# LoRA rows of the first conditioning layer fetched per batch row by indirect DMA onto quarters of the partitions, in place of masked expert tables

## The chip, the core and the metric

The program runs on one core of a Trainium2 chip, in one launch. The metric is device time in microseconds (us) of that core, from the first to the last instruction as the device counts it. The kernel before takes 626.87 us, the median of three runs (626.77 to 627.61).

## The reference, cut to what matters

`x` has 8 batch rows of 256 positions with 128 features. Two residual layers follow each other; each is a conditioning step and then a feed-forward block:

```
x = x + L0_ffn(L0_cond(x, itok_B_0_7))     # expert id 0..7 for each batch row
x = x + L1_ffn(L1_cond(x, itok_B_0_3))     # language id 0..3 for each batch row
```

The change touches `L0_cond` only. With D = 128, F = 512, rank 16 for the common and for each expert's part, and ALPHA = 2, it computes for a batch row b with expert e:

```
h = relu(x wi^T + 2 (x common_wi_a^T) common_wi_b^T + 2 (x experts_wi_a[e]^T) experts_wi_b[e]^T)
y =      h wo^T + 2 (h common_wo_a^T) common_wo_b^T + 2 (h experts_wo_a[e]^T) experts_wo_b[e]^T
```

`L0_ffn` is four rounds of a top-2 mixture of four experts (128 to 512 to 128, gelu), and it holds most of the arithmetic. `L1_cond` is a small LoRA by language, and `L1_ffn` is a gated block with two 512 x 512 layers.

## The kernel before

Activations lie with features on the 128 partitions and positions along the free axis, in four tiles t = 0..3 of 512 positions (`NT`), so that a tile holds two batch rows (`BPT`). All matrices are float32. A float32 matmul appears in the profile as two records ("passes"), each with its own weight load.

`L0_cond` does not multiply x by the low-rank factors one after the other. It makes merged dense weights for each batch row and multiplies by those:

- Common part, once: `pc_i` (L125) and `pc_o` (L130) multiply the common factors, contracting over 16 partitions; VectorE adds the dense weights and gives `wie` (L126) and `woe` (L131).
- Expert part: the factors of all eight experts lie below each other on 128 partitions (8 x 16 rows). `emask` (L110) is 2 where a partition belongs to the expert of batch row b and 0 elsewhere. VectorE masks the up table, eight times (`wam`, L146); GpSimd masks the down table, eight times (`wobm`, L162).
- `up_weights(b)` (L148): one matmul `pwi` (L150, contracting over 128 partitions, 512 columns) and one VectorE addition of `wie` (L152) give the up weights of one batch row. `down_weights(g)` (L160): four matmuls `pwo` (L165, 512 columns) and four additions (L168) give the down weights of four batch rows.
- `cond_up(t)` (L172) multiplies x by the up weights, two batch rows at 256 columns each for four chunks of 128 (`phc`, L178), and ScalarE applies relu. `cond_down(t)` (L185) sums four chunks for each batch row (`po`, L190), and VectorE copies the result to `cur[t]` (L194).

After that, `gate` (L199) computes the routing of a tile: `pg` matmuls (L207, L210), a chain of small VectorE operations with a tanh on ScalarE, transposes `pt` (L255) with the identity `ident`, and a broadcast on GpSimd (L261). `experts` (L264) runs the mixture for one tile and one round: `ph` (L269) with gelu (L273), and `py` (L283). Sixteen such steps follow each other, then the last layers.

What orders the work: each engine runs its instructions in one order fixed at build time. The tile framework assigns buffers from pools and inserts semaphore waits; a scheduler interleaves the instructions of neighbouring calls. PSUM (matmul results) is split into pools of 512-column banks: `ps_mm` with three, `ps_y` with two, `ps_bc` with two, `ps_g` with one. Loads are issued from the SyncE queue (SPq) and the ScalarE queue (ACTq). On GpSimd (POOL) the order at the start is: a memset of `ident`, a memset of the first `cwq`, an instruction of `masks.py:199` that reloads the library of GpSimd programs (it has no row of its own in the profile), the affine select that completes `ident`, the second `cwq`, the eight masks of L162, and then casts of later weights (L322).

Of the kernel before, what the change touches and what calls it, by code (L numbers as in the profile page):

```python
# [31 lines left out]

V_B1, V_B2, V_W1S, V_W2S, V_H1S, V_H2S, V_W3S, V_N = 0, 16, 20, 24, 28, 32, 36, 37

C_EIDX, C_PIDX, C_UPPER, C_N = 0, 1, 2, 18


@with_exitstack
def body(ctx: ExitStack, tc: tile.TileContext, a: dict, outT: bass.AP):

    nc = tc.nc

    w = ctx.enter_context(tc.tile_pool(name="w", bufs=1))
    act = ctx.enter_context(tc.tile_pool(name="act", bufs=1))
    hp = ctx.enter_context(tc.tile_pool(name="hp", bufs=9))
    mid = ctx.enter_context(tc.tile_pool(name="mid", bufs=2))
    small = ctx.enter_context(tc.tile_pool(name="small", bufs=3))
# [12 lines left out]
    xs = [act.tile([P, NT], F32, tag=f"x{t}", name=f"x{t}") for t in range(T)]  # L60
    ids = w.tile([P, 2 * B], I32, tag="ids", name="ids")
    nc.scalar.dma_start(ids, a["ids"].partition_broadcast(P))
    cst = load("cst", nc.scalar)
    waR = load("waR", nc.sync)
    wbT = load("wbT", nc.sync)
    cwia = load("cwia", nc.scalar)
    cwibT = load("cwibT", nc.scalar)
    wiT = load("wiT", nc.sync)
    nc.sync.dma_start(xs[0], a["xT"][:, ts(0, NT)])
    cwoa = load("cwoa", nc.scalar)  # L70
    cwobT = load("cwobT", nc.scalar)
    wobT = load("wobT", nc.sync)
    woaR = load("woaR", nc.sync)
    woT = load("woT", nc.sync)
    for t in range(1, T):
        nc.sync.dma_start(xs[t], a["xT"][:, ts(t, NT)])
    wg = load("wg", nc.scalar)
# [24 lines left out]
    for k in range(2):  # L102
# [2 lines left out]

    idf = w.tile([P, 2 * B], F32, tag="idf", name="idf")
    nc.vector.tensor_copy(idf, ids)

    emask = w.tile([P, B], F32, tag="emask", name="emask")
    nc.vector.tensor_scalar(  # L110
        emask, idf[:, 0:B], cst[:, C_EIDX : C_EIDX + 1], 2.0, ALU.is_equal, ALU.mult
    )
# [10 lines left out]
    wie = w.tile([P, F], F32, tag="wie", name="wie")  # L123
    pc = ps_mm.tile([P, NT], F32, tag="mm", name="pc_i")
    nc.tensor.matmul(pc, lhsT=cwia, rhs=cwibT, start=True, stop=True)  # L125
    nc.vector.scalar_tensor_tensor(wie, pc, 2.0, wiT, ALU.mult, ALU.add)  # L126
    woe = w.tile([P, FC, D], F32, tag="woe", name="woe")
    pc = ps_mm.tile([P, FC, D], F32, tag="mm", name="pc_o")
    for c in range(FC):
        nc.tensor.matmul(pc[:, c, :], lhsT=cwoa[:, ts(c, P)], rhs=cwobT, start=True, stop=True)  # L130
    nc.vector.scalar_tensor_tensor(woe, pc, 2.0, woT, ALU.mult, ALU.add)  # L131

    def masked(dst, src, mask, t):
        for b in range(BPT):
# [5 lines left out]


    cur = [act.tile([P, NT], F32, tag=f"cur{t}", name=f"cur{t}") for t in range(T)]
    wam = hp.tile([P, B, D], F32, tag="h", name="wam")
    wobm = hp.tile([P, B, D], F32, tag="h", name="wobm")
    for b in range(B):
        nc.vector.tensor_scalar(wam[:, b, :], waR, emask[:, b : b + 1], None, ALU.mult)  # L146

    def up_weights(b):  # L148
        pw = ps_bc.tile([P, F], F32, tag="bc", name=f"pwi_{b}")
        nc.tensor.matmul(pw, lhsT=wam[:, b, :], rhs=wbT, start=True, stop=True)  # L150
        wt = mid.tile([P, F], F32, tag="wib", bufs=3, name=f"wib_{b}")
        nc.vector.tensor_tensor(wt, pw, wie, ALU.add)  # L152
        return wt

    GB = 4
    down_w = [
        hp.tile([P, FC, GB, D], F32, tag="h", name=f"wob{g}") for g in range(B // GB)
    ]

    def down_weights(g):  # L160
        for b in range(g * GB, (g + 1) * GB):
            nc.gpsimd.tensor_scalar(wobm[:, b, :], wobT, emask[:, b : b + 1], None, ALU.mult)  # L162
        for c in range(FC):
            pw = ps_bc.tile([P, GB, D], F32, tag="bc", name=f"pwo_{g}_{c}")
            nc.tensor.matmul(  # L165
                pw, lhsT=woaR[:, ts(c, P)], rhs=wobm[:, ts(g, GB), :], start=True, stop=True
            )
            nc.vector.tensor_tensor(  # L168
                down_w[g][:, c], pw, woe[:, c, :].unsqueeze(1).to_broadcast([P, GB, D]), ALU.add
            )  # L170

    def cond_up(t):  # L172
        wt = [up_weights(t * BPT + b) for b in range(BPT)]
        h = hp.tile([P, FC, NT], F32, tag="h", name=f"hc_{t}")
        for c in range(FC):
            ph = ps_mm.tile([P, NT], F32, tag="mm", name=f"phc_{t}_{c}")
            for b in range(BPT):
                nc.tensor.matmul(  # L178
                    ph[:, ts(b, S)], lhsT=wt[b][:, ts(c, P)], rhs=xs[t][:, ts(b, S)],
                    start=True, stop=True,  # L180
                )
            nc.scalar.activation(h[:, c, :], ph, AF.Relu)  # L182
        return h

    def cond_down(t, h):  # L185
        po = ps_y.tile([P, NT], F32, tag="y", name=f"po_{t}")
        for b in range(BPT):
            g, k = divmod(t * BPT + b, GB)
            for c in range(FC):
                nc.tensor.matmul(  # L190
                    po[:, ts(b, S)], lhsT=down_w[g][:, c, k, :], rhs=h[:, c, ts(b, S)],
                    start=(c == 0), stop=(c == FC - 1),
                )
        nc.vector.tensor_copy(cur[t], po)  # L194
# [69 lines left out]
    def experts(r, t, cwb):  # L264
# [36 lines left out]
        if r == R - 1:  # L301
            nc.vector.tensor_tensor(xs[t], xs[t], cur[t], ALU.add)

    before = cond_up(0)
    for t in range(1, T):
        if t % (GB // BPT) == 1:
            down_weights(t // (GB // BPT))
        h = cond_up(t)
        cond_down(t - 1, before)
        before = h  # L310
    cwb = gate(0, 0)
# [160 lines left out]
def _laid_out(i):  # L472

    import numpy as np

    i = {k: np.asarray(v) for k, v in i.items()}

    def cols(v):
        return v.reshape(-1, P).T

    def rows(m):
        return m.reshape(-1, P, m.shape[1]).transpose(1, 0, 2)

    cst = np.zeros((P, C_N), np.float32)
    cst[:, C_EIDX] = np.arange(P) // 16
    cst[:, C_PIDX] = np.arange(P)
    cst[:, C_UPPER:] = np.triu(np.ones((E, E), np.float32), 1).reshape(-1)
    arrays = {
        "xT": i["x"].reshape(N, D).T,
        "ids": np.concatenate([i["itok_B_0_7"], i["itok_B_0_3"]]),  # L490
        "cst": cst,
        "wiT": i["L0_cond_wi"].T,
        "woT": rows(i["L0_cond_wo"].T),
        "cwia": i["L0_cond_common_wi_a"],
        "cwibT": i["L0_cond_common_wi_b"].T,
        "cwoa": i["L0_cond_common_wo_a"],
        "cwobT": i["L0_cond_common_wo_b"].T,
        "waR": i["L0_cond_experts_wi_a"].reshape(P, D),
        "wbT": i["L0_cond_experts_wi_b"].transpose(0, 2, 1).reshape(P, F),
        "woaR": i["L0_cond_experts_wo_a"].reshape(P, F),  # L500
        "wobT": i["L0_cond_experts_wo_b"].transpose(0, 2, 1).reshape(P, D),
        "wg": i["L0_ffn_Wg"].transpose(1, 0, 2),
        "bg": i["L0_ffn_bg"].reshape(-1),
        "W1": i["L0_ffn_W1"].transpose(1, 0, 2),
        "W2": i["L0_ffn_W2"].reshape(E, FC, P, D).transpose(2, 0, 1, 3),
        "laT": i["L1_cond_lora_A"].reshape(LR, D).T,
        "lbT": i["L1_cond_lora_B"].transpose(0, 2, 1).reshape(LR, D),
        "lemb": i["L1_cond_lang_embed"],
        "w1T": i["L1_ffn_w1_w"].T,
        "w2T": i["L1_ffn_w2_w"].T,  # L510
        "h1T": rows(i["L1_ffn_h1_w"].T),
        "h2T": rows(i["L1_ffn_h2_w"].T),
        "w3T": rows(i["L1_ffn_w3_w"].T),
        "vecs": np.concatenate(
            [
                cols(i["L0_ffn_b1"].reshape(-1)),
                cols(i["L0_ffn_b2"].reshape(-1)),
                cols(i["L1_ffn_w1_s"]),
                cols(i["L1_ffn_w2_s"]),
                cols(i["L1_ffn_h1_s"]),  # L520
                cols(i["L1_ffn_h2_s"]),
                cols(i["L1_ffn_w3_s"]),
            ],
            axis=1,
        ),
    }
    return {k: np.ascontiguousarray(v) for k, v in arrays.items()}
# [21 lines left out]
```

## Time and profile before

| what | value |
|---|---|
| median of three runs | 626.87 us |
| the profiled execution: device time | 628.72 us |
| the profiled execution: span from first to last instruction | 626.9 us |
| granted TensorE clock over the span | 0.990 |
| TensorE (PE) busy | 607.5 us, 97% |
| VectorE (DVE) busy | 242.7 us, 39% |
| ScalarE (ACT) busy | 229.4 us, 37% |
| GpSimd (POOL) busy | 93.7 us, 15% |
| DMA traffic | 8.81 MB, of it 7.44 MB in the first 60 us |

A row of a timeline starts with the start in us and the duration in us; then come engine, line, operation, output and inputs, shape and count; brackets say how long the engine was idle before and what ended that. A row that joins several instructions counts passes, so "pwi x4" is two matmuls. A duration of a single TensorE row includes the latency of the pipeline; in a stream the pace is shorter than the row. The chain of waits is followed back from the last instruction of the kernel and lists what the end had to wait for, piece after piece.

The page has PE at nine tenths or more in nearly every slice after the first, so there are two places where time can go: the start, before PE has its inputs, and the amount of PE work itself.

### The profile page before, as it was taken

What the parts mean: (1) busy time and instruction counts of PE and PEld (TensorE: products, weight loads), DVE (VectorE), ACT (ScalarE), POOL (GpSimd) and SP (SyncE); (2) the same over time, 40 slices, a digit from 0 to 9 for tenths busy, and PEclk for the clock granted to TensorE, in tenths of its full rate; (3) what the DMA queues carried; (4) which work ended last, traced back from release to release, by engine and by line L of the source; (5) the groups of instructions that cost most, each with busy time, mean ns of one, the idle gap of its engine ahead of it and who ended that gap; (6) DMA issues with size and microseconds to landing.
All of it is one profiled execution on the core that took longest, in us unless ns stands there. A gap on an engine that the chain in (4) does not pass through costs nothing.

```text
span 626.9 us, 4871 instructions
## 1 busy us (share of the span) xinstructions
PE 607.5 (97%) x1758; PEld 317.6 (51%) x1758; DVE 242.7 (39%) x563; ACT 229.4 (37%) x344; POOL 93.7 (15%) x137
## 2 busy tenths in 40 slices
PE   4999999999999999999999999999999998899996
PEld 2667444444444444444444444444444343678885
DVE  3355158614141432424141424224243314766533
ACT  0213443343333425344433334253433342365431
POOL 3302100211010101010100101010101000444421
PEclk9999999999999999999999999999999998799999
DMA  7600000000000000000000000000000000000001
GB/s 225 248 1 1 1 1 0 1 0 1 1 0 0 1 0 1 2 0 1 1 0 0 1 0 0 2 0 0 1 0 0 1 1 0 1 1 17 1 17 38
DMA packets 4131, 8.81 MB, mean 14 GB/s; under 512 B 1284, under 2 KB 1640, under 8 KB 3592
## 3 DMA queue, kind: packets, MB, share of 16 engines
q1 hardware_dynamic: 3256, 8.33, 3.8%
q8 instruction: 16, 0.26, 0.2%
q10 hardware_dynamic: 848, 0.14, 0.1%
q14 instruction: 11, 0.09, 0.0%
HBM read 7.41 MB, written 1.05 MB: 13 GB/s over the span
## 4 chain that ended last, share of the span: by engine, by line
PE 94%; DMA 1%; DVE 1%; ACT 1%; issue 1%; POOL 0%; ACTq 0%; DVEq 0%; POOLq 0%
PE ph L269 35%; PE py L283 35%; PE pha_True L402 5%; PE phb_True L402 4%; PE phc L178 2%; PE po L190 2%; PE p_True L402 2%; PE pwi L150 1%; PE pt L255 1%; PE pwo L165 1%; PE pg L210 1%; PE pout_True L402 1%; PE pg L207 1%; DMA woT<-in_woT_dram 1%; DMA cwibT<-in_cwibT_dram 1%; PE pv L355 1%
## 5 line engine op out<-in xcount | busy, mean ns | idle before, releaser
L273 ACT ACTIVATE h<-ph,vecs 128x512 f32<-128x512 f32 x256 | 175.7, 687 | 278.5 <-PE ph L269 275.8
L269 PE MATMUL ph<-cur,W 128*128 128x512 f32 x512 | 232.8, 596 | 0.4 <-ACT h L273 0.4
L283 PE MATMUL py<-h,W 128*128 128x512 f32 x512 | 227.7, 592 | 0.0
L283 PEld LDWEIGHTS py<-h,W 128*128 128x128 f32 x512 | 97.1, 190 | 121.5 <-issue 121.3
L269 PEld LDWEIGHTS ph<-cur,W 128*128 128x128 f32 x512 | 94.5, 190 | 109.4 <-issue 106.8
L288 DVE SCALAR_TENSOR_TENSOR tmp<-py,vecs,cwb 128x512 f32<-128x512 f32 x48 | 36.0, 751 | 203.7 <-PE py L283 203.7
L261 POOL PARTITION_BROADCAST cwb<-cwT x64 | 45.3, 811 | 403.3 <-DVE cwT L257 403.3
L288 DVE SCALAR_TENSOR_TENSOR acc<-py,vecs,cwb 128x512 f32<-128x512 f32 x16 | 12.0, 750 | 62.1 <-PE py L283 62.1
L292 DVE TENSOR_TENSOR acc<-acc,tmp 128x512 f32<-128x512 f32 x48 | 33.4, 695 | 1.2
L402 PE MATMUL pha_True<-h_True,h1S 128*128 128x512 f32 x128 | 31.4, 400 | 0.0
L402 PE MATMUL phb_True<-ha_True,h2S 128*128 128x512 f32 x128 | 30.9, 392 | 0.0
L402 PEld LDWEIGHTS pha_True<-h_True,h1S 128*128 128x128 f32 x128 | 24.6, 192 | 5.9
L402 PEld LDWEIGHTS phb_True<-ha_True,h2S 128*128 128x128 f32 x128 | 23.8, 188 | 6.2 <-ACT fhb_True L441 0.8
L182 ACT ACTIVATE hc<-phc 128x512 f32<-128x512 f32 x16 | 9.3, 596 | 34.4 <-PE phc L178 34.3
L389 POOL CAST h_True<-f 128x512 fp32r<-128x512 f32 x16 | 13.1, 823 | 45.7 <-DVE f L426 45.6
L207 PE MATMUL pg<-wg,chi 128*128 128x8 f32 x64 | 19.4, 324 | 0.0
L390 DVE TENSOR_TENSOR hb_True<-fhb_True,hb_True 128x512 fp32r<-128x512 f32 x16 | 12.0, 764 | 15.6 <-POOL hb_True L389 15.5
L421 ACT ACTIVATE g_True<-p_True,vecs 128x512 f32<-128x512 f32 x16 | 10.8, 688 | 19.8 <-PE p_True L402 19.7
L390 DVE TENSOR_TENSOR ha_True<-fha_True,ha_True 128x512 fp32r<-128x512 f32 x16 | 11.4, 717 | 15.2 <-POOL ha_True L389 15.2
L441 ACT ACTIVATE fhb_True<-phb_True,vecs 128x512 f32<-128x512 f32 x16 | 10.7, 688 | 15.8 <-PE phb_True L402 13.1
L441 ACT ACTIVATE fha_True<-pha_True,vecs 128x512 f32<-128x512 f32 x16 | 10.9, 689 | 15.1 <-PE pha_True L402 12.5
L257 DVE COPY cwT<-pt 128x512 f32<-128x512 f32 x16 | 11.1, 691 | 13.8 <-PE pt L255 13.8
(99 smaller groups left out, 401.0 us busy)
## 6 DMA issues: line engine op xcount, KB each, us to landing
W<-in_W_dram SPq DMA_DIRECT2D x2, 1024.0 KB, 9.7
x<-in_xT_dram SPq DMA_DIRECT2D x4, 256.0 KB, 5.7
h1T<-in_h1T_dram SPq DMA_DIRECT2D x1, 1024.0 KB, 9.2
h2T<-in_h2T_dram SPq DMA_DIRECT2D x1, 1024.0 KB, 9.2
out_dram<-o_True SPq DMA_DIRECT2D x4, 256.0 KB, 2.5
wbT<-in_wbT_dram SPq DMA_DIRECT2D x1, 256.0 KB, 3.9
wiT<-in_wiT_dram SPq DMA_DIRECT2D x1, 256.0 KB, 4.5
woaR<-in_woaR_dram SPq DMA_DIRECT2D x1, 256.0 KB, 3.0
```

The source lines that it names most:

```text
L178: nc.tensor.matmul(ph[:, ts(b, S)], lhsT=wt[b][:, ts(c, P)], rhs=xs[t][:, ts(b, S)], start=True, stop=True,)
L207: nc.tensor.matmul(pg[:, j, :], lhsT=chi[:, ts(j, P)], rhs=wg2[:, r, :], start=True, stop=False)
L261: nc.gpsimd.partition_broadcast(cwb[:, e, :], cwT[q : q + 1, :], channels=P)
L269: nc.tensor.matmul(ph, lhsT=W1[:, e, ts(c, P)], rhs=cur[t], start=True, stop=True)
L273: nc.scalar.activation(h[:, c, :], ph, AF.Gelu_apprx_tanh, bias=vecs[:, col : col + 1])
L283: nc.tensor.matmul(py, lhsT=W2[:, e, c, :], rhs=h[:, c, :], start=(c == 0), stop=(c == FC - 1))
L288: nc.vector.scalar_tensor_tensor(dst, py, vecs[:, col : col + 1], cwb[:, e, :], ALU.add, ALU.mult)
L292: nc.vector.tensor_tensor(acc, acc, dst, ALU.add)
L389: nc.gpsimd.tensor_copy(dst[0][:, c, :], full)
L390: nc.vector.tensor_tensor(dst[1][:, c, :], full, dst[0][:, c, :], ALU.subtract)
L402: nc.tensor.matmul(out, lhsT=wT[c], rhs=part[:, c, :], start=(c == 0 and k == 0), stop=(c == n - 1 and k == len(src) - 1),)
L441: nc.scalar.activation(full, ph, AF.Gelu, scale=vecs[:, col : col + 1])
```

## The change

The host lays each expert table with the 16 common rows below it: `wa` and `woa` and so on are 144 rows long, 128 rows of eight experts and 16 common ones. `idr` holds for each partition the expert id of the batch row to which its quarter belongs (partition quarter k of 32 belongs to batch row 4g + k). VectorE computes from it the row of the table that each partition wants (`rows`): on the first 16 partitions of a quarter a row of the expert, on the other 16 a common row. For each of the two groups g of four batch rows GpSimd issues four indirect DMAs, which fetch one row for each partition.

Merged weights are then made by matmuls that contract over one quarter of 32 partitions (expert and common part together), one quarter for each batch row, and VectorE computes 2 x product + dense weight in one operation. The masks (`emask`, `wam`, `wobm`), the common products (`pc_i`, `pc_o`) and `wie`, `woe` are gone. For the up weights there are four matmuls of 512 columns in a group; for the down weights there are sixteen of 128 columns. Each batch row has a PSUM bank of its own, from `ps_bc` and `ps_y`.

In the changed GpSimd order the eight indirect DMAs stand behind the affine select and so behind the reload of the library, and ahead of the second `cwq` memset. Loads of eight small or middle-sized tables leave the SyncE and ScalarE queues; `wiT` moves to the ScalarE queue, and `ids` stands later in it.

```
-    ids = w.tile([P, 2 * B], I32, tag="ids", name="ids")
-    nc.scalar.dma_start(ids, a["ids"].partition_broadcast(P))
-    cst = load("cst", nc.scalar)
-    waR = load("waR", nc.sync)
-    wbT = load("wbT", nc.sync)
-    cwia = load("cwia", nc.scalar)
...
+    idr = w.tile([P, B // GB], I32, tag="idr", name="idr")
+    nc.sync.dma_start(idr, a["idr"])
+    cst = load("cst", nc.scalar)
+    nc.sync.dma_start(xs[0], a["xT"][:, ts(0, NT)])
+    wiT = load("wiT", nc.scalar)
+    woT = load("woT", nc.sync)
+
+    rows = w.tile([P, B // GB], I32, tag="rows", name="rows")
+    nc.vector.tensor_scalar(
+        rows, idr, cst[:, C_STEP : C_STEP + 1], cst[:, C_BASE : C_BASE + 1], ALU.mult, ALU.add
+    )
+    lora = {}
+    for g in range(B // GB):
+        for name in ("wa", "wb", "woa", "wob"):
+            src = a[name]
+            t = w.tile([P, src.shape[1]], F32, tag=f"{name}{g}", name=f"{name}{g}")
+            nc.gpsimd.indirect_dma_start(
+                out=t, out_offset=None, in_=src,
+                in_offset=bass.IndirectOffsetOnAxis(ap=rows[:, g : g + 1], axis=0),
+                bounds_check=src.shape[0] - 1,
+            )
+            lora[name, g] = t
...
+    up_w, down_w = {}, {}
+    banks = [(ps_bc, "bc"), (ps_bc, "bc"), (ps_y, "y"), (ps_y, "y")]
+
+    def merged(g, which):
+
+        pw = []
+        for k, (pool, tag) in enumerate(banks):
+            pw.append(pool.tile([P, F], F32, tag=tag, name=f"pw{which}_{g}_{k}"))
+        if which == "i":
+            for k in range(GB):
+                q = slice(k * RK, (k + 1) * RK)
+                nc.tensor.matmul(
+                    pw[k], lhsT=lora["wa", g][q, :], rhs=lora["wb", g][q, :], start=True, stop=True
+                )
+        else:
+            for c in range(FC):
+                for k in range(GB):
+                    q = slice(k * RK, (k + 1) * RK)
+                    nc.tensor.matmul(
+                        pw[k][:, ts(c, P)], lhsT=lora["woa", g][q, ts(c, P)],
+                        rhs=lora["wob", g][q, :], start=True, stop=True,
+                    )
+        dense = wiT if which == "i" else woT.rearrange("p c d -> p (c d)")
+        for k in range(GB):
+            b = g * GB + k
+            wt = mid.tile([P, F], F32, tag=f"w{which}b", bufs=4, name=f"w{which}b_{b}")
+            nc.vector.scalar_tensor_tensor(wt, pw[k], 2.0, dense, ALU.mult, ALU.add)
+            (up_w if which == "i" else down_w)[b] = wt
...
+    merged(0, "i")
     before = cond_up(0)
+    merged(0, "o")
     for t in range(1, T):
-        if t % (GB // BPT) == 1:
-            down_weights(t // (GB // BPT))
+        if t == GB // BPT:
+            merged(1, "i")
         h = cond_up(t)
+        if t == GB // BPT + 1:
+            merged(1, "o")
         cond_down(t - 1, before)
         before = h
```

Below, `pwi` and `pwo` of the changed kernel are the matmuls of `merged` for the up and the down weights; group 0 and group 1 are the two groups of four batch rows; RK = 32 and GB = 4.

More of the change, by code (lines that the diff above doesn't have):

```diff
@@ L33 @@
 V_B1, V_B2, V_W1S, V_W2S, V_H1S, V_H2S, V_W3S, V_N = 0, 16, 20, 24, 28, 32, 36, 37
-C_EIDX, C_PIDX, C_UPPER, C_N = 0, 1, 2, 18
+C_EIDX, C_PIDX, C_UPPER, C_STEP, C_BASE, C_N = 0, 1, 2, 18, 19, 20
+RK = 32
+GB = P // RK
 @with_exitstack
@@ L60, in body @@
     xs = [act.tile([P, NT], F32, tag=f"x{t}", name=f"x{t}") for t in range(T)]
+    idr = w.tile([P, B // GB], I32, tag="idr", name="idr")
[19 more added lines that the diff above has]
+            lora[name, g] = t
     ids = w.tile([P, 2 * B], I32, tag="ids", name="ids")
     nc.scalar.dma_start(ids, a["ids"].partition_broadcast(P))
-    cst = load("cst", nc.scalar)
-    waR = load("waR", nc.sync)
-    wbT = load("wbT", nc.sync)
-    cwia = load("cwia", nc.scalar)
[L67 to L74, printed above, removed]
     for t in range(1, T):
@@ L107, in body @@
     nc.vector.tensor_copy(idf, ids)
[L109 to L112, printed above, removed]
     lmask = w.tile([LR, B], F32, tag="lmask", name="lmask")
@@ L120, in body @@
     )
[L123 to L131, printed above, removed]
     def masked(dst, src, mask, t):
@@ L142, in body @@
     cur = [act.tile([P, NT], F32, tag=f"cur{t}", name=f"cur{t}") for t in range(T)]
[L143 to L170, printed above, removed]
+    up_w, down_w = {}, {}
@@ L172, in cond_up @@
     def cond_up(t):
-        wt = [up_weights(t * BPT + b) for b in range(BPT)]
         h = hp.tile([P, FC, NT], F32, tag="h", name=f"hc_{t}")
@@ L178, in cond_up @@
                 nc.tensor.matmul(
-                    ph[:, ts(b, S)], lhsT=wt[b][:, ts(c, P)], rhs=xs[t][:, ts(b, S)],
+                    ph[:, ts(b, S)], lhsT=up_w[t * BPT + b][:, ts(c, P)], rhs=xs[t][:, ts(b, S)],
                     start=True, stop=True,
@@ L187, in cond_down @@
         for b in range(BPT):
-            g, k = divmod(t * BPT + b, GB)
             for c in range(FC):
                 nc.tensor.matmul(
-                    po[:, ts(b, S)], lhsT=down_w[g][:, c, k, :], rhs=h[:, c, ts(b, S)],
+                    po[:, ts(b, S)], lhsT=down_w[t * BPT + b][:, ts(c, P)], rhs=h[:, c, ts(b, S)],
                     start=(c == 0), stop=(c == FC - 1),
@@ L486, in _laid_out @@
     cst[:, C_PIDX] = np.arange(P)
-    cst[:, C_UPPER:] = np.triu(np.ones((E, E), np.float32), 1).reshape(-1)
+    cst[:, C_UPPER : C_UPPER + E * E] = np.triu(np.ones((E, E), np.float32), 1).reshape(-1)
+    own = np.arange(P) % RK < 16
+    cst[:, C_STEP] = 16 * own
+    cst[:, C_BASE] = np.arange(P) % 16 + np.where(own, 0, 8 * 16)
     arrays = {
@@ L493, in _laid_out @@
         "woT": rows(i["L0_cond_wo"].T),
[L494 to L501, printed above, removed]
+        "idr": np.repeat(i["itok_B_0_7"].reshape(B // GB, GB).T, RK, axis=0),
+        "wa": np.concatenate([i["L0_cond_experts_wi_a"].reshape(P, D), i["L0_cond_common_wi_a"]]),
+        "wb": np.concatenate(
+            [i["L0_cond_experts_wi_b"].transpose(0, 2, 1).reshape(P, F), i["L0_cond_common_wi_b"].T]
+        ),
+        "woa": np.concatenate([i["L0_cond_experts_wo_a"].reshape(P, F), i["L0_cond_common_wo_a"]]),
+        "wob": np.concatenate(
+            [i["L0_cond_experts_wo_b"].transpose(0, 2, 1).reshape(P, D), i["L0_cond_common_wo_b"].T]
+        ),
         "wg": i["L0_ffn_Wg"].transpose(1, 0, 2),
```

## The prediction

> **What bounds the kernel now.** I read the page first: TensorE (PE) is busy for 97% of the span, and the chain of waits is PE for 94%. So I asked the chain of waits, in order of time, for the first 75 us, where all of the change lies.
>
> ```profile
> 2.12 4.60 DMA cwibT<-in_cwibT_dram
> ...
> 6.74 4.69 DMA woT<-in_woT_dram
> ...
> 11.52 0.69 DVE woe L131
> 12.21 0.32 DVE wam L146
> 12.53 0.04 issue
> 12.58 3.78 PE pwi L150 x4
> 16.36 2.80 PE phc L178 x12
> ...
> 23.65 1.91 PE pwi L150 x4
> 25.56 3.64 PE phc L178 x16
> 29.20 3.45 PE po L190 x16
> ```
>
> Up to 12.58 us loads are the bound; from there PE runs without a gap worth naming up to 59.28, where the mixture (`ph` L269) begins. After that the change alters no PE work. So the new time is the old one plus the shift of that point: the start of the first `pwi`, plus what PE does between it and `ph`. The first four `pwi` passes go at 0.945 us each (3.78 / 4), later ones at 0.43 (1.72 / 4): PE starts at half pace and is up to speed near 16.4.
>
> GpSimd is idle in most of the span, but the timeline of its first 30 us matters, because the fetches go there.
>
> ```profile
> 0.86 0.53 POOL L103 MEMSET cwq<- 128x512 f32 x1
> 10.47 0.28 POOL masks.py:199 TENSOR_SCALAR_AFFINE_SELECT ident<-ident 128x128 f32<-128x128 f32 x1 [9.08 <-issue]
> 10.72 0.51 POOL L103 MEMSET cwq<- 128x512 f32 x1
> 11.23 4.76 POOL L162 TENSOR_SCALAR wobm<-wobT,emask 128x128 f32<-128x128 f32 x8
> ```
>
> Between 1.39 and 10.47 GpSimd does nothing: the library reload ahead of the affine select takes these 9.1 us. In the changed order all eight indirect DMAs stand behind that select.
>
> Last, two rows of the PE and weight-load timelines for matmuls that do not use the array as others do: `pll` (L351) fills 64 columns of it, `pc_i` contracts over 16 rows only.
>
> ```profile
> 463.46 1.07 PE L351 MATMUL pll<-x,laT 128*64 128x512 f32 x2
> 464.46 2.84 PE L269 MATMUL ph<-cur,W 128*128 128x512 f32 x6
> ```
>
> ```profile
> 6.86 2.04 PE L125 MATMUL pc_i<-cwibT,cwia 16*128 16x512 f32 x2 [6.86 <-DMA cwibT<-in_cwibT_dram]
> 8.70 1.91 PE L130 MATMUL pc_o<-cwobT,cwoa 16*128 16x128 f32 x8
> ```
>
> **Part 1: what is removed.** `emask`, `wam` (8 x 0.25 us of VectorE), `wobm` (4.76 us of GpSimd), `pc_i`, `pc_o`, `wie` and `woe` all lie before 12.58 or beside PE. What they set is the start of `pwi` at 12.58, and part 2 puts another start in its place; nothing more is gained from them. The eight L152 and eight L168 additions (0.69 us each) become sixteen `scalar_tensor_tensor` of one size with `wie`'s row (0.69): no change for VectorE.
>
> **Part 2: the fetch.** `rows` needs `idr` and `cst`, now first in their queues. In before `ids` had landed at 4.35 and `cst` at 5.35, so `rows` is ready near 5 and is hidden by the reload. GpSimd is free at 10.47 + 0.28 = 10.75. The first `pwi` needs two fetches, `wa` and `wb`. The trace has no DMA from GpSimd. Issuing one costs at least what the SyncE and ScalarE queues show (0.33 to 0.46 us); I set 2.5 us as the upper end, three times a broadcast (0.81 us), the nearest kind of GpSimd program here. Between them I take 1.0 us, close to the broadcast. Issue to landing of small and middle loads is 2.8 to 4.7 us in the DMA list (`wg` 2.8, `wbT` 3.9, `bg` 4.3, `woT` 4.7), and between 10 and 24 us the DMA engines are full (share 0.93 to 1.04, for W, h1 and h2 on SyncE's queue), so I take 3.6. First `pwi`: 10.75 + 2 x 1.0 + 3.6 = 16.3, that is +3.7 us. Bounds: 10.75 + 0.8 + 2.8 = 14.4 (+1.8), and 10.75 + 5.0 + 4.7 = 20.45 (+7.9). The start can't come out ahead of 12.58 unless the reload itself becomes shorter. The other six fetches are issued by 10.75 + 8 = 18.8 and landed by 23; `pwo` of group 0 needs its two at about 23, group 1 at about 33. They are covered by PE work; if issue costs 2.5 us, group 0's down factors (landed at 24.4) would still be nearly in time, since everything has moved back as well. GpSimd's casts L322 wait behind the fetches until 21, where w1T landed anyway.
>
> **Part 3: the matmuls of merging.** In before they are 8 `pwi` and 8 `pwo` of 512 columns, in the chain 9.13 + 7.17 = 16.30 us: 3.78 for the first pair and 12.52 after it. The change has the same number of columns: 8 `pwi` of 512, and 32 `pwo` of 128. Contracting over fewer rows saves nothing by itself: `pc_i` with 16 rows took 1.02 us a pass (2.04 / 2), the slow-pace `pwi` with 128 rows 0.945. What can save is that four quarters work at once. The Trainium skill (TensorE: Matmul & The Clock Gate, Part 3, Packing small matmuls) says that matmuls on different row groups run concurrently and gives 3.07 times for four at K = 32 and 512 columns; the same section says that matmuls start and end strictly in program order. By the figure, four `pwi` at full pace cost 8 x 0.43 / 3.07 = 1.1 us; by `pc_i`'s row, 3.43. But a float32 matmul here is two passes on the same quarter, which can't overlap each other. With order kept, only the second pass of one quarter and the first of the next can go together: five steps in place of eight, 5 x 0.43 = 2.15 us. I take that.
>
> For `pwo` a pass of 128 columns is as short as its weight load. The `pg` rows (8 columns, a new 128-column load each) follow each other at 0.11 us in the chain, so a load alone costs 0.11. If loads of different quarters go one after the other, 64 passes x 0.11 = 7.0 us, as before; if they overlap in pairs too, 2 x 17 steps x 0.11 = 3.7. I take 7.0: the only row near shows loads in series.
>
> Sum: the first group has four matmuls where a pair stood: four slow passes and one at full pace, 3.78 + 0.43 = 4.2, +0.4. After it, 2.15 + 7.0 = 9.2 against 12.52, -3.3.
>
> **Part 4: changing the shape of the array.** Here a rule of the skill speaks against the change: TensorEngine Tiling (Array Packing), Key Properties, says that changing the tiling mode drains TensorE. The `pll` row shows a price: its two passes start at 463.46, the next `ph` at 464.46, so 1.00 us for 2 x 0.43 = 0.86, and the weight load of `ph`, which otherwise lies beneath the matmul before, starts only there. That is 0.14, with its load of 0.11 up to 0.25; I take 0.2. In the changed PE order the array goes between 32 and 128 rows nine times (`pwi` to `phc`, to `pwo`, to `phc`, to `pwo`, to `phc`, then `pwi`, `phc`, `pwo`, `pg`): +1.8 us. Without the rule's cost it would be 0; with 0.25, 2.3.
>
> **Part 5: new waits on VectorE.** `phc` of tile 2 needs two evictions of group 1. Counted from the end of `po` 0: copy `cur` (0.69, from 0.25), `chi` (0.43), two evictions (1.38) end at 2.75, plus 0.2 to reach PE; PE's four `pwi` end at 2.15 + 0.2. PE waits 0.6, with `phc` and all behind it queued. At the end four evictions of group 1 (2.8 us) stand ahead of the gate's chain on VectorE; `pg`, two `ph` and the first `po` (0.9 + 1.7 + 3.4) cover all but some 0.3 ahead of `pt`. Given back: the ACT table load (1.28, with PE idle for 0.39 at 62) is issued under `po` now. Together +0.5; bounds 0 and 1.5.
>
> **The sum:** +3.7 + 0.4 - 3.3 + 1.8 + 0.5 = +3.1 us. The profiled span is 626.9, its device time 628.72, 1.8 more, and the median of unprofiled runs 626.87. I add the shift to the median: 630.0 us.
>
> **The rivals.**
>
> No overlap at all (the quarters queue up): first group four slow and four full passes, 5.5, +1.7; after it 3.44 + 7.0 = 10.4, -2.1; drains 1.8, start 3.7, waits 0.2: +5.3, 632.2 us. For it: `pc_i`'s row. Against it: the code gives each quarter its own bank and place. A fetch at 2.5 us each gives about the same: issue 3.0 us longer, 633. Both together pass 635. Chance of one of the two 0.25.
>
> Loads of quarters overlap in pairs as the passes do: `pwo` 3.7 in place of 7.0, waits 0.3 more: +0.1, 627.0. Chance 0.18.
>
> On the other side, faster: all four quarters run at once, both passes, loads included, as the 3.07 suggests. The first group then takes 1.9 slow, but `phc` must wait for two evictions (1.9 + 0.2 + 1.4 = 3.5), and PE stays slow for longer: +0.2. Group 1 is bound by VectorE at 2.95, `pwo` twice 0.9: 4.7 against 12.52, -7.8. With start 3.7, drains 1.8 and waits 0.8: -1.3, 625.6. It decides if four `pwi` of group 1 span less than 1.2 us; if the fetch is at its early end too, 623.7. Against it is the program order of passes. Chance 0.15.
>
> That the change does not do what it says: removing tables and masks was to free VectorE and GpSimd, and neither is what PE waits for after 12.58; this is contained in the sum.
>
> **How the numbers follow.** My forecast, pairs overlap and loads do not, has 0.42: 630.0, by its own bounds 627.5 to 633. 0.2% of the time is 1.25 us, about what a measurement can tell from no change. Slower by more: 0.42 x 0.95 + 0.25 = 0.65; faster by more: about half to two thirds of the last rival, with a few of the third, 0.14; within: 0.21. The range from 625.4 to 633.4 leaves out about one in ten on each side.
>
> **What would show it.** The first indirect DMA issued at about 10.8; its row about 1.0 us; `pwi` starting near 16.3; group 1's four `pwi` spanning near 2.2 us (3.4: no overlap; 1.1: full); each `pwo` group near 3.5 (1.8: loads overlap); gaps of about 0.2 at each change of shape; `ph` beginning about 3 us after 59.3. I am wrong if the library reload is no longer in front of the fetches or shorter, if a fetch costs a multiple of 1.0 us, or if four quarters overlap.

## The result, and the profile after

| | before | after |
|---|---|---|
| median, run beside each other (6 and 6 runs) | 627.26 us | 630.0 us (629.83 to 630.6) |
| ratio, 95% interval | | 1.0045 (1.0033 to 1.0058) |
| the same kernel again, later (11 and 7 runs) | 627.86 us | 629.81 us, ratio 1.0028 (1.0014 to 1.0041) |
| profiled execution: device time, span | 628.72, 626.9 us | 630.03, 627.7 us |
| PE busy | 607.5 us | 596.2 us |

The change makes the kernel slower by 0.45%, in the repetition by 0.28%. The predicted time was met to the first decimal. That was luck: the two largest terms of its sum were wrong and took each other away, so the sum is what this text is about. The shift itself was forecast at +3.1 us and measured at +2.7 and, in the repetition, +1.95; before came out 0.4 us above the 626.87 that the sum started from.

The chain of waits of the kernel after, for the stretch shown of before (start us, us, what):

```profile
10.51 0.28 POOL ident masks.py:199
...
11.01 1.38 POOL wa L81
...
12.69 7.82 DMA wb<-in_wb_dram,rows
...
20.64 2.10 PE pwi L152 x8
...
23.46 4.36 PE phc L175 x12
27.82 0.42 PE pwo L159 x4
28.24 1.06 PE phc L175 x4
29.30 1.09 PE pwo L159 x28
30.39 3.65 PE phc L175 x16
34.04 3.45 PE po L186 x16
37.49 1.90 PE pwi L152 x8
...
50.13 1.10 PE pwo L159 x32
...
67.87 3.43 PE py L279 x8
```

The fetch is the first half of it: the select ends at 10.79, the issue of `wa` and the gaps around it take until 12.69, where the issue of `wb` begins, and `wb` lands 7.82 us after that beginning. PE starts at 20.64 in place of 12.58. After that PE's merging, which the chain of before gave 16.30 us, is 2.10 + 1.90 + 2.61 us. The rows of `pwo` and of the first `py` in the chain of before are:

```profile
19.16 0.86 PE pwo L165 x2
20.02 0.86 PE phc L178 x4
20.88 2.77 PE pwo L165 x6
...
41.46 1.72 PE pwo L165 x4
...
43.97 1.82 PE pwo L165 x4
...
67.41 3.43 PE py L283 x8
```

GpSimd's timeline gives the price of an issue (start, us, row, in brackets the gap ahead of it):

```profile
11.01 1.38 POOL L81 DMA_INDIRECT wa<-in_wa_dram,rows  x1 [0.21 <-issue]
12.69 1.01 POOL L81 DMA_INDIRECT wb<-in_wb_dram,rows  x1 [0.30 <-issue]
14.01 1.01 POOL L81 DMA_INDIRECT woa<-in_woa_dram,rows  x1 [0.31 <-issue]
```

Each row is 1.01 us (the first 1.38), and the next begins 1.32 us after it began (after the first, 1.68).

### The profile page after: what moved, and what is told of

It reads as the page before. It is cut to its first block, busy times and chain, and to the rows that moved or that the text cites. A ratio compares the mean times of both kernels' runs of the same rounds, so it can differ in the third digit from the quotient of the medians.

```text
span 627.7 us, 4945 instructions
## 1 busy us (share of the span) xinstructions
PE 596.2 (95%) x1796; PEld 313.3 (50%) x1796; DVE 238.6 (38%) x553; ACT 230.0 (37%) x344; POOL 98.0 (16%) x137
## 3 DMA queue, kind: packets, MB, share of 16 engines
HBM read 7.99 MB, written 1.05 MB: 14 GB/s over the span
## 4 chain that ended last, share of the span: by engine, by line
PE 93%; issue 2%; DVE 1%; DMA 1%; POOL 1%; ACT 1%; POOLq 0%; DVEq 0%
PE ph L265 35%; PE py L279 35%; PE pha_True L402 5%; PE phb_True L402 4%; PE phc L175 3%; PE po L186 2%; PE p_True L402 2%; DMA wb<-in_wb_dram,rows 1%; PE pt L251 1%; PE pg L206 1%; PE pout_True L402 1%; PE pg L203 1%; PE pv L355 1%; PE pwi L152 1%; PE pll L351 1%
## 5 line engine op out<-in xcount | busy, mean ns | idle before, releaser
L152 PE MATMUL pwi<-wb,wa 32*128 32x512 f32 x16 | 4.1, 886 | 20.6 <-DMA wb<-in_wb_dram,rows 20.6
L175 PE MATMUL phc<-x,wib 128*128 128x256 f32 x64 | 16.7, 414 | 0.7 <-DVE wib L167 0.7
## 6 DMA issues: line engine op xcount, KB each, us to landing
h2T<-in_h2T_dram SPq DMA_DIRECT2D x1, 1024.0 KB, 12.8
```

What stands on the lines that cost most here:

```text
L175: nc.tensor.matmul(ph[:, ts(b, S)], lhsT=up_w[t * BPT + b][:, ts(c, P)], rhs=xs[t][:, ts(b, S)], start=True, stop=True,)
```

## Where the time went

Both profiled chains, cut at the same places (us; "predicted" joins the terms of the prediction that fall into a row):

| stretch | before | after | measured | predicted |
|---|---|---|---|---|
| start of the first `pwi` | 12.58 | 20.64 | +8.06 | +3.7 |
| first `pwi` to the first `phc` | 3.78 | 2.82 | -0.96 | +0.4 |
| the other merging, with its changes of shape and waits | 12.52 | 4.51 | -8.01 | -1.0 (-3.3 + 1.8 + 0.5) |
| `phc`, 64 passes | 14.58 | 16.35 | +1.77 | 0 |
| `pg` | 1.58 | 1.77 | +0.2 | 0 |
| sum, at `ph` | | | +1.07 | +3.1 |
| start of the first `py` | 67.41 | 67.87 | +0.46 | +3.1 |

(4.51 is 1.90 for the four `pwi` of group 1 and 0.42 + 1.09 + 1.10 for the 64 `pwo` passes. `ph` begins at 59.28 in before; in after at 62.17, less 1.82 for four `ph` passes that went ahead of `po`. Between `ph` and `py` before had PE idle for an ACT table load, which after issues earlier.)

The rows on `pwi` and `phc` have to be read together. PE's first matmuls go at half pace in both kernels: in before these are the four `pwi` passes (3.78 us where four take 1.72 later), in after the `pwi` of group 0 (2.10) and most of the first twelve `phc` (4.36 where before took 2.80). So the +1.77 is no new cost by itself; it has moved there from the row of `pwi`. From the first `pwi` to the end of the first twelve `phc` it is 6.58 us in before and 7.18 in after. How long the half pace lasts also differs between executions with the same PE work: the first twelve `phc` took 3.86 us in the control of before further down, and 4.94 in another execution of after. The first `py` follows (68.00 and 68.29).

So the changed part costs some 0.5 us, no more than such a variation, and the timed difference is 2.0 to 2.7 us. The rest lies in two places that the chain up to `py` does not show. One is outside the span: device time less span is 1.8 us in before and 2.2 to 2.5 in after. The other is the stretch near 525 us, in which the last layers begin and PE pauses. The windows of after there (start:end, length, busy us of PE, PEld, DVE, ACT, POOL, then the granted clock, DMA share and GB/s):

```profile
521.00:531.00 10.00, 7.89 (x15) 2.48 (x14) 5.54 (x10) 0.00 (x0) 0.00 (x0) 0.86 0.00 0
531.00:541.00 10.00, 8.40 (x23) 4.84 (x21) 6.20 (x10) 2.64 (x4) 3.69 (x5) 0.79 0.00 1
541.00:551.00 10.00, 9.13 (x33) 7.34 (x34) 7.83 (x11) 4.82 (x7) 4.31 (x7) 0.83 0.01 2
```

The control experiment, which is before with another source of `ident`, has 0.97, 0.84 and 0.85 there. The granted clock loses 5.2 us of 30 in the one and 3.4 in the other (10 us times what lacks to 1.00). From the first `py` to the end it is 559.8 and 558.1 us, for the same code. Every profile of this study has a tail of one of two lengths: 558.0 to 558.4 in six of them, where the clock loses 3.4 us over the 30 us that begin 453 us after the first `py`, and 559.3 to 559.9 in the other six, where it loses 5.1 or 5.2. The profiled execution of before has the long one too (559.5; clock 0.88, 0.84, 0.76), so the profiled pair differs by 1.3 us only. By their spans, before's other runs (median 625.8) mostly have the short tail and after's mostly the long one. So some 1 us of the timed difference goes with the granted clock after PE's pause, in code that the change does not touch. What decides between the two lengths, and what the 0.6 us outside the span is, stays open.

## The experiments

Theory A: the start is the price of the fetch (the 9 us in which GpSimd does nothing ahead of the select, read as a library reload; then issues; then a landing that queues behind the big loads), and the four quarters of the array, weight loads included, work at the same time. Rival B: quarters overlap in pairs only, as predicted, and the gain comes from elsewhere (the shorter contraction, fewer products, other order). Each experiment changes the kernel after, where nothing else is said. The first four ran together beside 9 runs of before (median 627.52), the next four beside 35 (627.56), the last two beside 11 (627.86).

### The identity loaded as data, so that the fetches come first

```
-    make_identity(nc, ident)
+    nc.scalar.dma_start(ident, a["ident"])
```

> The changed kernel, with the identity loaded from memory on the ScalarE queue in place of the affine select, so that no library reload stands ahead of the fetches. Theory (the fetch is late because it stands behind the reload of 9.1 us): the first indirect DMA is issued near 3.2 us in place of 11.0, wb lands between 10 and 14, the first pwi starts there in place of 20.6, and the time falls by 6.5 to 10 us, to 620 to 623.5. Rival (the fetch waits for something else, or the first DMA of this kind is slow to start wherever it stands): pwi stays near 20 and the time at 630.

617.12 us (616.08 to 619.49), ratio 0.9845 (0.9823 to 0.9866). GpSimd's first fetch is issued at 3.34, the first `pwi` starts at 8.88, and the first `py` at 57.12, 10.75 ahead of after. The chain shows what is bound next:

```profile
7.67 8.80 DMA wob<-in_wob_dram,rows
...
16.60 0.49 PE pwo L159 x4
```

The fourth fetch lands at 16.47, and PE waits 0.48 us for it. With the fetches first the change makes the kernel faster than before. The issue of `wb` begins 7.67 us earlier (5.02 for 12.69) and PE starts 11.76 us earlier, so the early fetch escapes most of the queue as well. The control is the same edit in the kernel before:

> The kernel before, with the identity loaded as data in place of the affine select, so that GpSimd's library reload of 9.1 us is gone there too. Nothing is left out. Theory (the reload costs only because the fetches stand behind it): the first pwi of before waits for woT and the products made from it at 12.58 us, which the reload does not touch, so the time stays within 0.2% of before, near 627.0. Rival (part of the 10 us that loading the identity brought to the changed kernel has nothing to do with the fetches, such as a reload that also slows the DMA queues or the later casts): faster here as well, by 2 us or more, 625 or less.

627.82 us (626.64 to 629.67, 21 runs), ratio 1.0003 (0.9996 to 1.0011): no change, as the theory has it. But the run is not what I had expected it to be. GpSimd's wait of 9 us is still there, now ahead of the masks:

```profile
10.74 4.77 POOL L162 TENSOR_SCALAR wobm<-wobT,emask 128x128 f32<-128x128 f32 x8 [9.03 <-issue]
```

So the wait does not belong to the identity: it stands ahead of the select in the one kernel and of the masks in the other, and the fetches of the run above went ahead without it. No row shows what fills it, so that it is a library reload is not shown by the profile. What the control does show is that the edit alone is worth nothing in before, and that nobody waits for GpSimd at that time:

```profile
6.30 4.79 DMA woT<-in_woT_dram
11.18 0.69 DVE woe L131
...
12.12 3.78 PE pwi L150 x4
15.90 3.86 PE phc L178 x12
```

Whether a kernel before that has no such wait at all would be faster, this run leaves open. The same 9 us are free in the one kernel and, with the queue that the fetches then meet, cost 10.75 us at the first `py` in the other, by what stands behind them in GpSimd's order.

### The big loads held back

```
-    W1 = load("W1", nc.sync, hp, "h")
-    W2 = load("W2", nc.sync, hp, "h")
+    def held(name, pool=w, tag=None):
+        t = pool.tile(list(a[name].shape), F32, tag=tag or name, name=name)
+        nc.vector.tensor_copy(t[(slice(None),) + (0,) * (len(t.shape) - 2) + (slice(0, 1),)], lora["wb", 0][:, 0:1])
+        nc.sync.dma_start(t, a[name])
+        return t
+
+    W1 = held("W1", hp, "h")
+    W2 = held("W2", hp, "h")
...
+    h1T = held("h1T")
+    h2T = held("h2T")
```

> The changed kernel with the loads of W1, W2, h1T and h2T (4 MB) held back until wb of group 0 has landed. Theory (7.9 us from issue to landing of wb are queueing behind these loads on the same DMA engines): wb lands about 3 us after its issue, pwi starts near 15.7 in place of 20.6, and the time falls by 5 us to 625. Rival (an indirect DMA of 128 rows takes about 8 us by itself): pwi at 20.6, time 630.

625.05 us (624.76 to 625.61), ratio 0.9962 (0.9949 to 0.9976). GpSimd is as late as in after, but:

```profile
12.56 3.41 DMA wb<-in_wb_dram,rows
...
16.10 2.10 PE pwi L158 x8
...
18.92 5.49 PE phc L181 x12
```

3.41 us in place of 7.82, the value that the prediction assumed (3.6), and PE starts at 16.10 (predicted 16.3). So the 4.4 us are queueing behind W1, W2, h1T and h2T. With the start as predicted the kernel is faster than before. PE starts 4.54 us ahead of after, but the first `py` only 3.22 (64.65), because the half pace lasts longer here (`phc` 5.49 us in place of 4.36).

### Plain loads in place of the fetches

Rows 0 to 127 of each table, loaded by SyncE. This leaves out the choice of rows by expert.

```
-            nc.gpsimd.indirect_dma_start(
-                out=t, out_offset=None, in_=src,
...
+            nc.sync.dma_start(t, src[0:P, :])
```

> The changed kernel with the eight tables loaded by plain DMAs of rows 0 to 127 on the SyncE queue in place of the indirect ones; the choice of rows by expert id is left out. This takes the whole price of the fetch away and keeps the matmuls. Theory (fetch costs 8 us of start, the overlap gives 7 back, the rest is even): pwi starts at 8 to 9 us, the time falls by 11 to 12 us to 618 to 619. Rival (something of the change other than the fetch makes it slow, such as the switches of array shape or the waits on VectorE): the time stays above 624.

617.23 us (616.73 to 619.47), ratio 0.9843 (0.9825 to 0.9861); `pwi` starts at 7.99. Fetching by GpSimd, with the 9 us of waiting and the queue, costs 12.8 us against a plain load, and the rest of the change is worth 10.3 us against before: 4.6 of it by an earlier start (7.99 for 12.58, as `pwi` no longer stands behind `woT`, `woe` and the masks), most of the rest by merging on quarters.

### Four matmuls on one quarter

All four matmuls of a group read quarter 0, in both places; this leaves out the weights of the other three batch rows.

```
-                q = slice(k * RK, (k + 1) * RK)
+                q = slice(0, RK)
```

> The changed kernel with all four matmuls of a group reading the first quarter of the partitions, so that no two can be in the array at once; the weights of the other three batch rows are left out (they get the first one's). Theory (the four quarters run at once, in both passes and with their weight loads): four pwi at full pace then take 3.4 us, a group of pwo 3.4 to 3.5 in place of 1.1, the first group is longer by 2 to 3; time up by about 7 us, to 637. Rival (what became short is the matmul that contracts over 32 rows): pwi and pwo as they were, 630. By my prediction on record (pairs overlap, weight loads in series) pwo would not change and the time would go up by about 2.5 us, to 632.5.

643.39 us (642.72 to 644.8), ratio 1.0254 (1.0237 to 1.027): slower by 13.4 us than after, where 7 was expected. The chain:

```profile
20.76 7.16 PE pwi L152 x8
27.92 5.42 PE phc L175 x12
...
35.05 3.32 PE pwo L159 x28
...
45.47 3.62 PE pwi L152 x8
...
59.65 3.76 PE pwo L159 x32
...
64.61 3.30 PE ph L265 x4
```

Contracting over 32 rows saves nothing: 7.16 and 3.62 us for eight passes are close to what before pays for passes over 128 rows at half and at full pace (8 x 0.945 and 8 x 0.43). The 2.10, 1.90 and 1.10 us of after come from quarters that work together, and B falls. Two things I had not expected. The first group costs 5.06 us more and not 2 to 3, since all eight passes follow each other at half pace. And at the end, after 3.76 us of quarter matmuls `ph` runs at half pace (3.30 us in place of 1.82). In this run matmuls on one quarter neither brought PE to full pace (after 7.16 us of them `phc` is still slow at 5.42) nor kept it there. Of the 13.9 us by which the first `py` is later than in after (81.74), the rows of `pwi` and `pwo` hold 11.9; `phc` (+0.9) and `ph` (+1.5) at half pace account for the rest, less the waits that PE no longer has.

### PE brought to full pace ahead of time

```
+    for k in range(12):
+        nc.tensor.matmul(pwarm, lhsT=xs[0][:, 0:P], rhs=xs[0], start=True, stop=True)
     merged(0, "i")
```

> The changed kernel with twelve full matmuls of 512 columns on x ahead of the first pwi; their result is used by nobody, and they end by about 20 us, while PE would wait for the fetch. Nothing is left out. Theory (PE at half pace in the first 7 us of its work is a term of its own): the first pwi start at about 20.6 as before, go at full pace (1.05 us in place of 2.10), the first twelve phc passes take 2.8 us in place of 4.36, and the next phc are a little shorter; in all 2.5 to 3 us less, 627.2. Rival (the first phc are slow because they wait for weights or evictions, or because of what the DMA queues do): no change, 630.

626.43 us (624.25 to 628.07, 14 runs), ratio 0.9978 (0.9967 to 0.9989). The timeline of PE:

```profile
6.06 13.42 PE L302 MATMUL pwarm<-x 128*128 128x512 f32 x24 [6.06 <-DMA x<-in_xT_dram]
20.40 1.14 PE L152 MATMUL pwi<-wb,wa 32*128 32x512 f32 x8 [0.93 <-DMA wb<-in_wb_dram,rows]
22.27 3.02 PE L175 MATMUL phc<-x,wib 128*128 128x256 f32 x12 [0.73 <-issue]
```

`pwi` and `phc` go at full pace (1.14 and 3.02 in place of 2.09 and 4.36), and the first `py` starts at 65.35, 2.5 us ahead of after, as expected. The other 1.1 us of the measured 3.6 lie behind the first `py`; the profiled run has the short tail (558.1 us). So the half pace is a term of its own, worth 2.5 us where PE's first needed matmuls pay it. It is not a cost that only the change has: before pays 2.06 us in its first four `pwi` passes (3.78 for 1.72).

### The parts together

Identity loaded and big loads held, by the two edits above:

> The changed kernel with both of the earlier edits that shorten the fetch: the identity loaded as data, and the four big loads (W1, W2, h1T, h2T) held until wb of group 0 has landed. Nothing is left out. Theory (the landing time is queueing behind those loads): wb lands 3.4 us after its issue in place of 6.4, so the first pwi start near 8.2 in place of 8.9, and wob lands near 11.5 in place of 16.5, so PE no longer waits for it with its first pwo: about 2 us less than with the identity alone, 615. Rival (GpSimd's fetches queue behind each other, not behind the loads): wob still lands near 16.5, and the time stays at 617.

620.67 us (617.81 to 621.69), ratio 0.9873 (0.9852 to 0.9893): 3.5 us worse than without holding, where 2 us better was expected. PE no longer waits for `wob`, but that gains nothing: at half pace (5.33 us) the twelve `phc` end at 17.01, later than the 16.60 at which `wob` let `pwo` begin without holding. And PE loses more later. Two timelines of it show why; VectorE:

```profile
27.45 2.09 DVE L204 CAST chi<-cur 128x512 fp32r<-128x512 f32 x1
29.47 1.27 DVE L173 SCALAR_TENSOR_TENSOR wib<-pwi,wiT 128x512 f32<-128x512 f32 x2
```

and GpSimd:

```profile
27.37 1.90 POOL L328 CAST h2S<-h2T 128x2048 fp32r<-128x2048 f32 x1 [0.59 <-DMA h2T<-in_h2T_dram]
```

`chi` starts 0.08 us after GpSimd's cast and ends 0.27 after it, in 2.09 us where 0.43 is its time elsewhere. The evictions of `pwi` stand behind it, PE waits 1.65 us for them, and the sixteen `phc` after that take 5.38 us in place of 3.83, at a granted clock of 0.71. The Trainium skill (SBUF — State Buffer, "SBUF: two separate sides") says that a VectorE operation in a two-port mode and a GpSimd operation share a pair of ports as an exclusive lock, not a share of bandwidth. The rows agree: `chi` does not slow down in proportion, it waits. In the run with the identity alone it began 1.34 us into a cast of GpSimd, and again it ended 0.27 us after that cast:

```profile
27.11 0.83 DVE L198 CAST chi<-cur 128x512 fp32r<-128x512 f32 x1
```

```profile
25.77 1.90 POOL L322 CAST h1S<-h1T 128x2048 fp32r<-128x2048 f32 x1 [1.87 <-DMA h1T<-in_h1T_dram]
```

Which mode `chi` runs in no row shows. To test the wait, the casts of GpSimd were made to wait until the last up weights of group 1 are written:

```
+            nc.vector.tensor_copy(sh[:, 0:1], up_w[B - 1][:, 0:1])
             nc.gpsimd.tensor_copy(sh, full)
```

> The kernel with the identity loaded and the big loads held, and one thing more: GpSimd's five casts (L328 there) wait until the last of group 1's up weights is written, by a copy of one column from it into each target. Nothing is left out. In the run without this, chi took 2.09 us in place of 0.43 while GpSimd cast h2T, PE waited 1.65 us for the evictions behind it and the next phc went at 5.38 us for sixteen passes in place of 3.83. Theory (VectorE's cast waits for GpSimd's, and PE loses its pace in the wait): chi is back at 0.43, the wait is gone, sixteen phc take 3.83 us, first py near 57.1 in place of 60.26, time near 617.5. Rival (chi is long for another reason, such as DMA writes into the same memory, or PE's pace falls whatever the wait): chi and the wait stay, 620.7.

618.08 us (617.2 to 619.99, 4 runs), ratio 0.9854 (0.9839 to 0.987). VectorE and PE:

```profile
27.80 0.43 DVE L204 CAST chi<-cur 128x512 fp32r<-128x512 f32 x1
```

```profile
28.93 3.84 PE L181 MATMUL phc<-x,wib 128*128 128x256 f32 x16
```

`chi` is at 0.43, the wait is gone, `phc` is at 3.84, and the first `py` starts at 57.41 in place of 60.26. That is where the 3 us were. Holding the loads gains nothing at this point (617.12 without it), since the first twelve `phc` still take 5.49 us. The best version has the identity loaded, the big loads held and four matmuls on a tile of ones while PE waits:

```
+    nc.vector.memset(cur[3], 1.0)
...
+    for k in range(4):
+        nc.tensor.matmul(pwarm, lhsT=cur[3][:, 0:P], rhs=cur[3], start=True, stop=True)
     merged(0, "i")
```

> The changed kernel with the identity loaded, the big loads held, and four full matmuls on a tile of ones (result used by nobody) from about 1.5 to 7.5 us, so that PE is at full pace when the fetched rows come. Nothing is left out. If start, queueing and half pace are separate terms, they add up: first pwi near 8.2 at 1.05 us in place of 2.1, first twelve phc near 2.8 in place of 4.4 to 5.5, in all 2.5 us below the run without these matmuls, 612.5. Rival (the half pace at the start depends on time since the program's start and not on PE's work, or the first pwo then waits for wob anyway): no better than 615.

614.27 us (614.02 to 617.78), ratio 0.9806 (0.9785 to 0.9828), faster than before and after. Its PE timeline:

```profile
1.44 6.54 PE L309 MATMUL pwarm<-cur 128*128 128x512 f32 x8 [1.44 <-DVE ones L344]
8.97 1.14 PE L159 MATMUL pwi<-wb,wa 32*128 32x512 f32 x8 [1.00 <-DMA wb<-in_wb_dram,rows]
10.85 3.02 PE L182 MATMUL phc<-x,wib 128*128 128x256 f32 x12 [0.73 <-DVE wib L174]
```

The `pwi` are early and at full pace, and the first `py` starts at 53.93. `chi` begins at 24.31, between two casts of GpSimd, and takes 0.43 us; nothing in the program keeps it clear of them. 612.5 was expected: `pwi` came at 8.97 and not at 8.2, which is 0.8 of the 1.8 us, because holding the loads gains nothing for `wb` where it is issued that early: it landed 3.51 us after its issue at 5.04, and without holding `pwi` came at 8.88. (The 6.4 us from which the gain was expected are the DMA list's median over the fetches of both groups.)

### The kernel after once more

> The changed kernel once more, unaltered, for the spread of its runs. If the 1.4 us that its span has beyond what is seen at the first py, and the 0.6 us outside the span, belong to it: median 630.0, span 627.6, 2.4 outside. If the first part is chance from run to run: median near 628.6, with single runs between 627.5 and 630.5.

629.81 us (628.77 to 630.75), spans from 626.4 to 628.4 with a median of 627.4, and 2.2 to 2.5 us outside. The 0.6 us outside the span came back with this kernel; the tail was again the long one in the profiled run (559.3 us), and single spans vary by 2 us. How much of the tail is chance stays open.

## Why the number was right and the sum was not

**The start (+3.7; measured +8.06).** The steps were right in kind: GpSimd's wait stands ahead of the fetches (select free at 10.79, predicted 10.75), then come issues, then a landing. The sizes were not. The list's "issue to landing" begins with the issue, as `woT` in before shows (6.74 plus 4.69 is its landing in the chain), so 2 x 1.0 + 3.6 counts the issue of `wb` twice; counted once, one issue of 1.0 and a landing of 3.6 stand against 1.90 (the issue of `wa` with its gaps) and 7.82. The start of 16.10 with the loads held meets the predicted 16.3 by these two errors: 0.9 too little for the issue, 1.0 counted twice. The step that failed is the landing. I had written that the DMA engines are full between 10 and 24 us and then took the landing time of loads issued when the queues were empty. The small loads that before issues behind the large ones (`laT` 10.0 and `lbT` 9.2 us, 32 KB each) were the nearer rows, and a landing like theirs would have given more than the bound. 3.41 us with the loads held shows that the excess is queueing and not the kind of DMA. My upper bound, +7.9, was just passed.

**The matmuls of merging (-2.9 with the first group; measured -8.97 with all changes of shape and waits).** The failed step is "with order kept, only the second pass of one quarter and the first of the next can go together". In the trace of the best version four `pwi` passes lie within 0.71 us from 8.97 on, and the other four follow from 9.48 (two windows of its timeline):

```profile
8.97 0.71 PE L159 MATMUL pwi<-wb,wa 32*128 32x512 f32 x4 [1.00 <-DMA wb<-in_wb_dram,rows]
```

```profile
9.48 0.64 PE L159 MATMUL pwi<-wb,wa 32*128 32x512 f32 x4
```

Passes on one quarter follow each other (3.62 us for eight, 0.45 each), so four in the array at once are on four quarters, and eight take 1.14 us in place of 3.62: 3.2 times, near the 3.07 that the Trainium skill (TensorE: Matmul & The Clock Gate, Part 3, Packing small matmuls) gives and that I had set aside. Weight loads overlap as well: 32 `pwo` passes of 128 columns, each with its load, took 1.10 us where one quarter takes 3.76. "The only row near shows loads in series" was true and was no evidence, since that row (`pg`) loads the whole array. The rival on the faster side had this mechanism and its sizes (`pwo` 0.9 a group; 1.10 measured). Its test, four `pwi` of group 1 under 1.2 us, fails as it was put: 1.90. But some 0.8 of that (against 1.14 in the warmed runs) is a wait for the bank that VectorE's `cur` copy frees, not work.

**Changes of shape (+1.8).** The size was somewhat low. The 64 `pwo` passes cost 0.42 + 1.09 us in two stretches and 1.10 in one, so the two further changes of shape cost 0.41 there, and the four `phc` between them 0.20 more than in before (1.06 for 0.86): some 0.3 each, where 0.2 was taken. These costs are contained in the 4.51 us and in the rows of `phc` and `pg`, which is why this term is not on top of the measured gain.

**Waits on VectorE (+0.5).** There are waits, in other places than forecast: 0.73 us ahead of the first `phc`, and the bank at `pwi` of group 1. They are contained in the same rows. The pause for the ACT table load went as predicted.

**What the sum lacked.** I had let the half pace end with the first `pwi`, as it did in before. The `pwi` of after took 2.10 us in place of 4.2, and the half pace went on through `phc`; so the stretch to the end of the first twelve `phc` came out at +0.6, near the forecast of +0.4, by two errors and a wait of 0.7 for VectorE. And the span's tail and the time outside it, together some 1.5 to 2 us, no argument from the first 70 us could give. So 630.0 was right by cancellation: 4.4 us too little for the start, 8.4 too much for merging, 1.8 for pace and some 2 elsewhere not foreseen.

## What to carry to other kernels

Before moving work to another queue, read what stands ahead of it there and how full the DMA engines are when it is issued; here a wait of 9 us and a queue of 4.4 us took back a gain of some 10 us. Matmuls on separate quarters of the array do run together, float32 passes and weight loads included; and PE's first matmuls go at half pace, which cost some 2.5 us here, and nothing where other matmuls took it while PE waited for loads. When an engine off the path becomes free earlier, ask what its next instructions collide with.

## What the hardware showed that was not expected

- Half pace at the start does not show as a lower granted clock: in after the clock reads 1.00 from 20 to 28 us, while passes take twice their time. In the run with one quarter it does show later (0.72 from 62 to 68 us).
- Matmuls on a single quarter did not bring PE to full pace in the one run that has them. The Trainium skill (TensorE: Matmul & The Clock Gate, Part 1) says that activity within a window of some 3.4 us opens the clock; here 7.16 us of them, gapless, did not, and the 12 `phc` after them took 5.42 us. The eight full-size passes ahead of `pwi` in the best version, too, took 6.54 us (0.82 each, where full pace is 0.43), so most of that stretch was at half pace.
- An indirect DMA of 128 rows keeps GpSimd for 1.01 us, whether a row has 128 or 512 columns, and the next follows after 1.32 us; it landed 3.4 us after issue beside light traffic and 7.8 beside four megabytes of other loads.
